# Recommendation scorer on one core: transposes of a pair of chunks in one PSUM tile of two banks, pooled sums copied by two pairs, one store at the end

## Chip, core and metric

The kernel runs on one core of one Trainium2 chip. The metric is device time in microseconds (us), the median of four executions. The engines are called as in the profile: PE is TensorE's matmuls and PEld its weight loads, DVE is VectorE, ACT is ScalarE, POOL is GpSimd, SP is SyncE. Beside the times there is one execution taken with the profiler, and every line of the trace is from that one.

## What is computed

A user has 69 item fields, a candidate item is the label, and both are rows of a table `emb` of 100001 x 96 floats. For every one of 16384 users:

```python
u = emb[batch_user]                       # 69 rows of 96
ql = emb[batch_label[:, 0]]               # 1 row
q = jnp.broadcast_to(ql[:, None, :], u.shape)
z = jnp.concatenate([q, u, q - u, q * u], axis=-1)
h = _dice(z @ W1 + b1, a1, EPS_DICE)      # 384 -> 64
h = h @ W2 + b2
att = h @ W3 + b3                         # one weight a field
eff = (batch_user < ITEM_NUM)[..., None]
pre = jnp.where(eff, u * att, 0.0)
pooled = jnp.einsum('gf,bfe->bge', window, pre).reshape(u.shape[0], G * E)   # 10 groups of fields
x = jnp.concatenate([pooled, ql], axis=-1)
h = _dice(_bn_eval(x @ Wf1 + bf1, EPS_BN), af1, EPS_DICE)                    # 1056 -> 200
h = _dice(_bn_eval(h @ Wf2 + bf2, EPS_BN), af2, EPS_DICE)                    # 200 -> 80
return h @ Wf3 + bf3
```

`_dice(x, a)` is `(a * (1 - p) + p) * x` with `p` the sigmoid of `x`.

## The kernel before

**Tiling.** The users are cut into 32 blocks of 512. Of the 69 fields, 64 are "main" and 5 are "tail". A chunk is 512 (user, field) places: a main chunk holds 8 users with all their 64 main fields, a tail chunk one tail field of all 512 users. A block has 64 main and 5 tail chunks. The loop runs over pairs of chunks, 69 x 32 / 2 = 1104 of them, and the order of all instructions is written by hand (`tc.manual_schedule()`); each engine runs its own instructions in that order and waits on semaphores for the others.

**A pair's way through the steps.** In step i:

- `seed(i-1)` (L278 to L295): a bf16 matmul of zeros opens a PSUM tile `ph`, and ACT copies into it the part of the hidden layer that depends on the label alone.
- `pool(i-8)` (L367 to L393): per chunk four matmuls with `u` as the stationary side and the attention weights `rw` as the moving one give the pooled sums `acc` in PSUM; DVE copies them into `pooled`. The `acc` tile exists once, so a pair's matmuls wait for the copy of the pair before.
- every fourth step `attend_rows` (L337, `prow`), and a step later `spread` (L353 `patt`, then DVE `w` at L356 and `rw` at L359) turn hidden values of four pairs into attention weights. Tail chunks go through `attend_tail` (L346, L347) instead.
- `hidden(i-2)` (L326 to L330): eight matmul records of `uT` and `quT` into `ph`, then sigmoid and an affine step on ACT and the product `y` on DVE.
- `fetch(i)` (L298 to L320): eight indirect DMAs by POOL (`gather`, L227) bring 128 rows each into `u`; PE transposes each (`ptr`, L308), four to a PSUM bank; per chunk DVE multiplies the bank by the label's row into `quT` (L311, for tail chunks L318) and ACT copies it into `uT` (L319).
- planned extra work: the loads of the next block's indices, its label's rows, and the dense tower of the block before in ten parts (`top1` L406 to L413 in eight, `top2` L420 to L424, `top3` L429 to L432, which also stores 512 results from SP's queue).

**Buffers.** `u` has 14 buffers (`upool`), `uT` and `quT` five each, `ps_tr` two banks, `ps_h` two, `ps_x` two, `ps_acc` one, `ps_m` one: eight PSUM banks in all. A gather needs its `u` buffer free, which is last read by `pool` eight steps after the fetch.

**Order in fetch.** A transpose is written straight after its gather, and each waits for that one gather:

```python
for t in range(4):
    gather(u[:, 4 * j + t, :], rows[n][:, 4 * k + t : 4 * k + t + 1])
    nc.tensor.transpose(ptr[:, t * P : (t + 1) * P], u[:, 4 * j + t, :], ident)
```

On POOL only gathers are queued, 8 for each pair and 4 more for each block's labels, 8960 in all.

Of the kernel before, what the change touches and what calls it, by code (L numbers as in the profile page):

```python
# [30 lines left out]
F32 = mybir.dt.float32  # L31
BF16 = mybir.dt.bfloat16
I32 = mybir.dt.int32
AF = mybir.ActivationFunctionType
ALU = mybir.AluOpType
PSUM = bass.MemoryType.PSUM

P = 128
B, F, E, G = 16384, 69, 96, 10
# [24 lines left out]
def rec_kernel(  # L64
# [23 lines left out]
    nc = tc.nc  # L88

    const = ctx.enter_context(tc.tile_pool(name="const", bufs=1))  # L90
# [7 lines left out]
    xpool = ctx.enter_context(tc.tile_pool(name="xpool", bufs=1))  # L98
# [31 lines left out]
    qTs = []  # L130
    for i in range(2):
        t = const.tile([E + 1, BLK + NS], F32, name=f"qT{i}")
# [47 lines left out]
    wf3 = const.tile([D2, 1], F32, name="wf3")  # L180
# [5 lines left out]
    bf3c = column(bf3, "bf3c", 1)  # L186
# [12 lines left out]

    with tc.tile_pool(name="prep_ps", bufs=1, space=PSUM) as pps:  # L200
        pv = pps.tile([P, E], F32, name="pv")
# [17 lines left out]
    def tail_weights(f):  # L219
        nc.vector.tensor_scalar_mul(V[:, f, :], wf1[:, 0, :], wr[:, f, 0:1])  # L220
        for g in range(1, G):
            nc.vector.scalar_tensor_tensor(
                V[:, f, :], wf1[:, g, :], wr[:, f, g : g + 1], V[:, f, :], ALU.mult, ALU.add
            )

    def gather(dst, index):
        nc.gpsimd.indirect_dma_start(  # L227
            out=dst,
            out_offset=None,
            in_=emb,  # L230
            in_offset=bass.IndirectOffsetOnAxis(ap=index, axis=0),
        )

    def chunk(c):

        return divmod(c, NCH)
# [33 lines left out]

    def by_field(ap):

        return ap.rearrange("e (s o) -> e s o", o=1).to_broadcast([ap.shape[0], NS, FM])

    def seed(i):

# [21 lines left out]
    def fetch(i):  # L298

        u = upool.tile([P, 8, E], F32, tag="u", name=f"u{i}")  # L300
        uT = tpool.tile([E, 2, 512], F32, tag="uT", name=f"uT{i}")
        quT = tpool.tile([E, 2, 512], F32, tag="quT", name=f"quT{i}")
        for j in range(2):
            n, k = chunk(2 * i + j)
            ptr = ps_tr.tile([E, 512], F32, tag="tr", name=f"ptr{i}_{j}")
            for t in range(4):
                gather(u[:, 4 * j + t, :], rows[n][:, 4 * k + t : 4 * k + t + 1])
                nc.tensor.transpose(ptr[:, t * P : (t + 1) * P], u[:, 4 * j + t, :], ident)  # L308
            q = qTs[n % 2][0:E]
            if k < NMAIN:  # L310
                nc.vector.tensor_tensor(  # L311
                    quT[:, j, :].rearrange("e (s f) -> e s f", f=FM),
                    ptr.rearrange("e (s f) -> e s f", f=FM),
                    by_field(q[:, k * NS : (k + 1) * NS]),
                    ALU.mult,
                )
            else:
                nc.vector.tensor_tensor(quT[:, j, :], ptr, q[:, 0:BLK], ALU.mult)  # L318
            nc.scalar.copy(uT[:, j, :], ptr)  # L319
        return u, uT, quT  # L320

    def hidden(i, ph, uT, quT):
# [19 lines left out]
    def attend_tail(i, j, y, uT):  # L342
# [3 lines left out]
        nc.tensor.matmul(pa, vrep[j * H1 : (j + 1) * H1, :], y[j * H1 : (j + 1) * H1, :], start=True, stop=True)  # L346
        nc.vector.scalar_tensor_tensor(pres[n][:, k - NMAIN, :], pa, bb[0:E], uT[:, j, :], ALU.add, ALU.mult)  # L347

    def spread(b, row):
# [14 lines left out]
        )  # L364
        return rw

    def pool(i, u, rw):  # L367

        todo = [(j, *chunk(2 * i + j)) for j in range(2)]
        todo = [(j, n, k) for j, n, k in todo if k < NMAIN]  # L370
        if not todo:
            return
        pa = ps_acc.tile([E, 2, NS, G], F32, tag="acc", name=f"acc{i}")
        for j, n, k in todo:
            for t in range(4):
                nc.tensor.matmul(  # L376
                    pa[:, j, 2 * t : 2 * t + 2, :].rearrange("e n g -> e (n g)"),
                    u[:, 4 * j + t, :],
                    rw[:, i % 4, j, t, :],
                    start=True,  # L380
                    stop=True,
                )
        if len(todo) == 2:
            _, n, k = todo[0]
            nc.vector.tensor_copy(  # L385
                pooled[n][:, :, k * NS : (k + 2) * NS].rearrange("e g s -> e s g"),
                pa.rearrange("e j s g -> e (j s) g"),
            )
        else:
            j, n, k = todo[0]  # L390
            nc.vector.tensor_copy(
                pooled[n][:, :, k * NS : (k + 1) * NS].rearrange("e g s -> e s g"), pa[:, j]
            )  # L393

    KTOP = G + 1 + NTAIL
# [29 lines left out]
        return x2  # L425

    def top3(n, x2):
        p3 = ps_m.tile([1, BLK], F32, tag="m", name=f"p3_{n}")
        nc.tensor.matmul(p3, wf3, x2, start=True, stop=True)  # L429
        res = xpool.tile([1, BLK], F32, tag="res", name=f"res{n}")  # L430
        nc.vector.tensor_scalar(res, p3, bf3c, None, ALU.add)
        nc.sync.dma_start(out=out_v[n : n + 1], in_=res)  # L432

    out_v = out.rearrange("(n b) o -> n (o b)", n=NBLK)

    cs, pooled, pres, x1s, x2s, qs, us, hs, phs, ys, bands, rws, p1s = ({} for _ in range(13))

# [32 lines left out]
    with tc.manual_schedule():  # L470
        qs[0] = head_gather(0)
        head_turn(0, qs.pop(0))
        cs[0] = head_row(0)
        for i in range(NPAIR + POOL_LAG + 16):
            if 0 <= i - 1 < NPAIR:
                phs[i - 1] = seed(i - 1)
            if 0 <= i - POOL_LAG < NPAIR:
                k = i - POOL_LAG
                pool(k, us.pop(k), rws[k // 4])
                if k % 4 == 3:  # L480
                    rws.pop(k // 4)
            if 0 <= i - 3 < NPAIR and (i - 3) % 4 == 3:
                b = (i - 3) // 4
                bands[b] = attend_rows(b, [ys[4 * b + k] for k in range(4)])
            if 0 <= i - 3 < NPAIR:
                k = i - 3
                uT = hs.pop(k)[0]
                for j in range(2):
                    if chunk(2 * k + j)[1] >= NMAIN:
                        attend_tail(k, j, ys[k], uT)  # L490
            if 0 <= i - 4 < NPAIR and (i - 4) % 4 == 3:
                b = (i - 4) // 4
                rws[b] = spread(b, bands.pop(b))
# [12 lines left out]
            for work in plan.pop(i, []):  # L506
                work()
    assert not plan


# [45 lines left out]
```

## Time and profile before

| what | us |
|---|---|
| median of four executions | 11338.62 |
| lowest, highest | 11337.48, 11348.81 |
| profiled execution, its own time | 11343.88 |
| its span, first to last instruction | 11342.1 |
| PE busy, idle waiting for gathered rows at L308 | 9833.1, 1292.8 |
| POOL busy | 8529.2 |
| DVE busy, ACT busy | 3191.8, 3761.1 |
| mean granted TensorE clock | 0.699 |

A line of costly groups reads: line, engine, operation, out<-in, shapes and count, then busy time and mean ns of one, then the idle time of the engine just before these instructions and what ended most of it. "Issue" is time in which an engine waited for nothing that the profile shows. A line of the timeline reads: start, duration, engine, line, operation, names, shapes, count, and in brackets the idle time before it with the one that ended it. A matmul of fp32 leaves two records, a transpose one.

Three groups that the change touches, from the costliest groups of the page:

```profile
L319 ACT COPY uT<-ptr 96x512 f32<-96x512 f32 x2208 | 1283.3, 581 | 2328.6 <-DVE quT L311 2151.6
...
L311 DVE TENSOR_TENSOR quT<-ptr,qT 96x512 f32<-96x512 f32 x2048 | 1352.6, 679 | 720.1 <-PE ptr L308 715.1
L385 DVE COPY pooled<-acc 96x160 f32<-96x160 f32 x1008 | 433.2, 430 | 2251.9 <-PE acc L376 2250.6
```

ACT spends 2151.6 us idle before the copies of `ptr`, until the DVE product of the same bank is done, since the two read one after the other.

### The profile page before, as it was taken

Reading aid. Unit: us, or ns where it says so; the run is one execution under the profiler, and the core shown is the slowest. Engines: PE = TensorE matmul, PEld = TensorE weight load, DVE = VectorE, ACT = ScalarE, POOL = GpSimd, SP = SyncE. Lnnn points to the kernel's source line nnn. Section 1 sums busy time; section 2 is a strip of 40 time slices with the busy share of each in tenths; the row PEclk is TensorE's granted clock in tenths of the full one; section 3 lists DMA queues with packets and bytes.
Section 4 is the critical chain, followed back from the end, with each engine's and each line's share of the span. In section 5 each row is a group of like instructions: output and inputs, shape, how many; then the busy total and the mean of one; then the engine's idle time right before and its main releaser. Section 6 shows DMA issues by size and latency. Waiting matters only on the chain.

```text
span 11342.1 us, 108113 instructions
## 1 busy us (share of the span) xinstructions
PE 9833.1 (87%) x41348; PEld 4777.8 (42%) x41348; DVE 3191.8 (28%) x5424; ACT 3761.1 (33%) x6086; POOL 8529.2 (75%) x8966
## 2 busy tenths in 40 slices
PE   7888888888888888888888888888888888888888
PEld 3444444444444444444444444444444444444444
DVE  3222222222222222222222222222222222222222
ACT  2333333333333333333333333333333333333332
POOL 7777777777777777777777777777777777777775
PEclk6766777667776677766767667777677766777767
DMA  1111111111111111111111111111111111111111
GB/s 44 40 41 40 40 40 40 40 40 40 40 40 40 40 40 40 40 40 40 40 40 40 40 40 40 40 40 40 40 40 40 40 40 40 40 40 40 40 40 29
DMA packets 295008, 453.59 MB, mean 40 GB/s; under 512 B 145952, under 2 KB 151104, under 8 KB 294496
## 3 DMA queue, kind: packets, MB, share of 16 engines
q0 software_dynamic: 286720, 440.98, 16.2%
q8 instruction: 331, 5.42, 0.2%
q1 hardware_dynamic: 6142, 4.77, 0.2%
q14 instruction: 181, 1.48, 0.0%
q10 hardware_dynamic: 1634, 0.94, 0.0%
HBM read 446.04 MB, written 0.07 MB: 39 GB/s over the span
## 4 chain that ended last, share of the span: by engine, by line
PE 33%; POOL 33%; DMA 18%; issue 12%; ACT 2%; DVE 1%; POOLq 0%; ACTq 0%
POOL u L227 32%; DMA u<-in_emb,rows 18%; PE ph L326 11%; PE acc L376 9%; PE p L406 4%; PE ptr L308 3%; PE prow L337 2%; PE ph L278 2%; POOL q L227 1%; ACT y L329 1%; PE pa L346 1%; PE patt L353 1%; DVE y L330 1%; ACT y L328 1%; PE pc L267 0%
## 5 line engine op out<-in xcount | busy, mean ns | idle before, releaser
L227 POOL DMA_INDIRECT u<-in_emb,rows x8832 | 8407.5, 952 | 2691.5 <-issue 2267.9
L308 PE MATMUL ptr<-ident,u 128*96 128x128 f32 x8832 | 2080.8, 358 | 1306.3 <-DMA u<-in_emb,rows 1292.8
L308 PEld LDWEIGHTS ptr<-ident,u 128*96 128x96 f32 x8832 | 1238.9, 157 | 3253.6 <-DMA u<-in_emb,rows 1679.5
L376 PEld LDWEIGHTS acc<-rw,u 128*96 128x96 f32 x16384 | 2073.9, 220 | 507.5 <-issue 506.9
L376 PE MATMUL acc<-rw,u 128*96 128x20 f32 x16384 | 2185.8, 284 | 1.8 <-DVE rw L359 1.3
L319 ACT COPY uT<-ptr 96x512 f32<-96x512 f32 x2208 | 1283.3, 581 | 2328.6 <-DVE quT L311 2151.6
L330 DVE TENSOR_TENSOR y<-ph,y 128x512 f32<-128x512 f32 x1104 | 763.7, 692 | 4443.3 <-ACT y L329 4341.6
L328 ACT ACTIVATE y<-ph 128x512 f32<-128x512 f32 x1104 | 659.2, 597 | 3855.9 <-PE ph L326 3855.6
L326 PE MATMUL ph<-uT,A 96*64 96x512 f32 x4416 | 1812.7, 913 | 0.0
L326 PE MATMUL ph<-quT,w 96*64 96x512 f32 x4416 | 1701.5, 861 | 0.0
L311 DVE TENSOR_TENSOR quT<-ptr,qT 96x512 f32<-96x512 f32 x2048 | 1352.6, 679 | 720.1 <-PE ptr L308 715.1
L385 DVE COPY pooled<-acc 96x160 f32<-96x160 f32 x1008 | 433.2, 430 | 2251.9 <-PE acc L376 2250.6
L329 ACT ACTIVATE y<-y,a1c,na1c 128x512 f32<-128x512 f32 x1104 | 897.4, 813 | 36.6
L326 PEld LDWEIGHTS ph<-quT,w 96*64 96x64 f32 x4416 | 448.1, 196 | 1088.5 <-issue 1088.5
L281 ACT COPY ph<-cT 128x512 f32<-128x512 f32 x1008 | 591.2, 586 | 449.0 <-PE ph L278 447.1
L278 PE MATMUL ph<-zrow 1*128 1x512 bf16 x1104 | 529.3, 479 | 163.4 <-DVE y L330 161.3
L406 PE MATMUL p<-pooled,wf 96*100 96x512 f32 x1280 | 665.3, 665 | 1.2 <-DVE x L410 0.8
L326 PEld LDWEIGHTS ph<-uT,A 96*64 96x64 f32 x4416 | 284.1, 178 | 540.8 <-issue 451.3
L337 PE MATMUL prow<-y,v 128*32 128x512 f32 x2208 | 443.9, 889 | 0.0
L339 ACT COPY row<-prow 128x512 f32<-128x512 f32 x276 | 161.5, 585 | 596.5 <-PE prow L337 595.2
L406 PEld LDWEIGHTS p<-pooled,wf 96*100 96x100 f32 x1280 | 233.9, 192 | 289.1 <-issue 286.9
L278 PEld LDWEIGHTS <-zrow 1*128 1x128 bf16 x1104 | 104.1, 94 | 477.1 <-issue 453.0
(71 smaller groups left out, 2651.0 us busy)
## 6 DMA issues: line engine op xcount, KB each, us to landing
u<-in_emb,rows POOLq DMA_INDIRECT x8832, 2.4
ids<-in_idx SPq DMA_DIRECT2D x32, 140.0 KB
q<-in_emb,ids POOLq DMA_INDIRECT x128, 2.4
wf<-in_Wf ACTq DMA_DIRECT2D x1, 825.0 KB
out<-res SPq DMA_DIRECT2D x32, 2.0 KB
w<-in_W SPq DMA_DIRECT2D x1, 96.0 KB
wf<-in_Wf ACTq DMA_DIRECT2D x1, 62.5 KB
a1c<-in_a SPq DMA_DIRECT2D x2, 0.2 KB
```

The source lines that it names most:

```text
L227: nc.gpsimd.indirect_dma_start(out=dst, out_offset=None, in_=emb, in_offset=bass.IndirectOffsetOnAxis(ap=index, axis=0),)
L278: nc.tensor.matmul(ph, zrow[:, 0:P], zrow, start=True, stop=False)
L308: nc.tensor.transpose(ptr[:, t * P : (t + 1) * P], u[:, 4 * j + t, :], ident)
L311: nc.vector.tensor_tensor(quT[:, j, :].rearrange("e (s f) -> e s f", f=FM), ptr.rearrange("e (s f) -> e s f", f=FM), by_field(q[:, k * NS ...
L319: nc.scalar.copy(uT[:, j, :], ptr)
L326: nc.tensor.matmul(ph[j * H1 : (j + 1) * H1, :], w, x[:, j, :], start=False, stop=last)
L328: nc.scalar.activation(y, ph, AF.Sigmoid, scale=S_DICE)
L329: nc.scalar.activation(y, y, AF.Identity, bias=a1c, scale=na1c)
L330: nc.vector.tensor_mul(y, ph, y)
L337: nc.tensor.matmul(pr[32 * k : 32 * (k + 1), :], v2, y, start=True, stop=True)
L376: nc.tensor.matmul(pa[:, j, 2 * t : 2 * t + 2, :].rearrange("e n g -> e (n g)"), u[:, 4 * j + t, :], rw[:, i % 4, j, t, :], start=True, st ...
L406: nc.tensor.matmul(p1, w[:, h * DH : (h + 1) * DH], x, start=(k == 0), stop=(k == KTOP - 1))
```

## The change

All eight gathers of a pair are written first, then the eight transposes into one PSUM tile `ptr` of two banks, of which there is now one (`ps_tr` has one buffer of two banks instead of two of one). The first transpose waits for all eight gathers through dependencies added by hand; the others have no wait. One DVE product and one ACT copy read both banks; only where a pair lies in two blocks or has a main and a tail chunk are there two DVE products.

`pool` opens an `acc` tile at even pairs, writes the next pair's sums beside it, and copies both at the odd pair, as one DVE copy for each block they belong to.

`top3` makes its 512 results with `x2` as the stationary side, four matmuls of one column each, into 4 columns of a tile `res` of 128 x 128 in SBUF that holds all results. `store()` at the end transposes `res`, copies it and stores all 16384 results in one DMA. The bias `bf3` is loaded broadcast to 128 partitions.

```diff
+    bf3c = const.tile([P, 1], F32, name="bf3c")
+    nc.sync.dma_start(out=bf3c, in_=bf3.rearrange("(o n) -> o n", o=1).to_broadcast([P, 1]))
+    res = const.tile([P, NBLK * NQ], F32, name="res")
...
-    ps_tr = ctx.enter_context(tc.tile_pool(name="ps_tr", bufs=2, space=PSUM))
+    ps_tr = ctx.enter_context(tc.tile_pool(name="ps_tr", bufs=1, space=PSUM))
...
+        sources = []
         for j in range(2):
             n, k = chunk(2 * i + j)
-            ptr = ps_tr.tile([E, 512], F32, tag="tr", name=f"ptr{i}_{j}")
             for t in range(4):
-                gather(u[:, 4 * j + t, :], rows[n][:, 4 * k + t : 4 * k + t + 1])
-                nc.tensor.transpose(ptr[:, t * P : (t + 1) * P], u[:, 4 * j + t, :], ident)
...
+                sources.append(gather(u[:, 4 * j + t, :], rows[n][:, 4 * k + t : 4 * k + t + 1]))
+        ptr = ps_tr.tile([E, 2, 512], F32, tag="tr", name=f"ptr{i}")
+        for t in range(8):
+            turn = nc.tensor.transpose(
+                ptr.rearrange("e j x -> e (j x)")[:, t * P : (t + 1) * P], u[:, t, :], ident
+            )
+            if t == 0:
+
+                for source in sources[1:]:
+                    tc.add_manual_dep(turn.ins, source.ins.name, SYNC)
+        (n0, k0), (n1, k1) = chunk(2 * i), chunk(2 * i + 1)
+        q = qTs[n0 % 2][0:E]
+        if n0 == n1 and k1 < NMAIN:
+            nc.vector.tensor_tensor(
+                quT.rearrange("e j (s f) -> e (j s) f", f=FM),
+                ptr.rearrange("e j (s f) -> e (j s) f", f=FM),
+                by_field(q[:, k0 * NS : (k0 + 2) * NS]),
+                ALU.mult,
+            )
...
+        nc.scalar.copy(uT, ptr)
         return u, uT, quT
...
+        if i % 2 == 0:
+            accs[0] = ps_acc.tile([E, 4, NS, G], F32, tag="acc", name=f"acc{i}")
+        pa = accs[0]
+        for j in range(2):
+            if chunk(2 * i + j)[1] < NMAIN:
+                for t in range(4):
+                    nc.tensor.matmul(
+                        pa[:, 2 * (i % 2) + j, 2 * t : 2 * t + 2, :].rearrange("e n g -> e (n g)"),
...
+        if i % 2 == 0:
             return
...
+        for block in sorted({n for n, k in places if k < NMAIN}):
+            m = [m for m, (n, k) in enumerate(places) if n == block and k < NMAIN]
+            k = places[m[0]][1]
             nc.vector.tensor_copy(
+                pooled[block][:, :, k * NS : (k + len(m)) * NS].rearrange("e g s -> e s g"),
+                pa[:, m[0] : m[-1] + 1].rearrange("e m s g -> e (m s) g"),
             )
...
     def top3(n, x2):
-        p3 = ps_m.tile([1, BLK], F32, tag="m", name=f"p3_{n}")
-        nc.tensor.matmul(p3, wf3, x2, start=True, stop=True)
-        res = xpool.tile([1, BLK], F32, tag="res", name=f"res{n}")
-        nc.vector.tensor_scalar(res, p3, bf3c, None, ALU.add)
-        nc.sync.dma_start(out=out_v[n : n + 1], in_=res)
...
+        p3 = ps_m.tile([P, NQ], F32, tag="m", name=f"p3_{n}")
+        for k in range(NQ):
+            nc.tensor.matmul(p3[:, k : k + 1], x2[:, k * P : (k + 1) * P], wf3, start=True, stop=True)
+        nc.vector.tensor_scalar(res[:, n * NQ : (n + 1) * NQ], p3, bf3c, None, ALU.add)
+
+    def store():
+        p4 = ps_m.tile([NBLK * NQ, P], F32, tag="m", name="p4")
+        nc.tensor.transpose(p4, res, ident)
+        r = xpool.tile([NBLK * NQ, P], F32, tag="g1", name="r")
+        nc.vector.tensor_copy(r, p4)
+        nc.sync.dma_start(out=out.rearrange("(m p) o -> m (p o)", p=P), in_=r)
```

More of the change, by code (lines that the diff above doesn't have):

```diff
@@ L35 @@
 ALU = mybir.AluOpType
+SYNC = mybir.DependencyInfo(mybir.DependencyClass.Sync, mybir.DependencyReason.DATA)
 PSUM = bass.MemoryType.PSUM
@@ L185, in rec_kernel @@
     af2c = column(af2, "af2c", D2)
-    bf3c = column(bf3, "bf3c", 1)
+    bf3c = const.tile([P, 1], F32, name="bf3c")
+    nc.sync.dma_start(out=bf3c, in_=bf3.rearrange("(o n) -> o n", o=1).to_broadcast([P, 1]))
+    res = const.tile([P, NBLK * NQ], F32, name="res")
     naf1c = [one_minus(t, f"naf1c{i}") for i, t in enumerate(af1c)]
@@ L226, in gather @@
     def gather(dst, index):
-        nc.gpsimd.indirect_dma_start(
+        return nc.gpsimd.indirect_dma_start(
             out=dst,
@@ L271, in by_field @@
     def by_field(ap):
-        return ap.rearrange("e (s o) -> e s o", o=1).to_broadcast([ap.shape[0], NS, FM])
+        return ap.rearrange("e (s o) -> e s o", o=1).to_broadcast([ap.shape[0], ap.shape[1], FM])
     def seed(i):
@@ L302, in fetch @@
         quT = tpool.tile([E, 2, 512], F32, tag="quT", name=f"quT{i}")
+        sources = []
         for j in range(2):
             n, k = chunk(2 * i + j)
-            ptr = ps_tr.tile([E, 512], F32, tag="tr", name=f"ptr{i}_{j}")
             for t in range(4):
-                gather(u[:, 4 * j + t, :], rows[n][:, 4 * k + t : 4 * k + t + 1])
[L308 to L318, printed above, removed]
@@ L319, in fetch @@
-            nc.scalar.copy(uT[:, j, :], ptr)
+                sources.append(gather(u[:, 4 * j + t, :], rows[n][:, 4 * k + t : 4 * k + t + 1]))
[7 more added lines that the diff above has]
+                    tc.add_manual_dep(turn.ins, source.ins.name, SYNC)
@@ new lines, in fetch @@
+        (n0, k0), (n1, k1) = chunk(2 * i), chunk(2 * i + 1)
[7 more added lines that the diff above has]
+            )
+        elif n0 == n1 and k0 >= NMAIN:
+            nc.vector.tensor_tensor(
+                quT, ptr, q[:, 0:BLK].rearrange("e (o x) -> e o x", o=1).to_broadcast([E, 2, BLK]), ALU.mult
+            )
+        else:
+            for j, (n, k) in enumerate([(n0, k0), (n1, k1)]):
+                q = qTs[n % 2][0:E]
+                if k < NMAIN:
+                    nc.vector.tensor_tensor(
+                        quT[:, j, :].rearrange("e (s f) -> e s f", f=FM),
+                        ptr[:, j, :].rearrange("e (s f) -> e s f", f=FM),
+                        by_field(q[:, k * NS : (k + 1) * NS]),
+                        ALU.mult,
+                    )
+                else:
+                    nc.vector.tensor_tensor(quT[:, j, :], ptr[:, j, :], q[:, 0:BLK], ALU.mult)
@@ L365, in spread @@
         return rw
+    accs = {}
     def pool(i, u, rw):
-        todo = [(j, *chunk(2 * i + j)) for j in range(2)]
-        todo = [(j, n, k) for j, n, k in todo if k < NMAIN]
-        if not todo:
-            return
[L373 to L384, printed above, removed]
-            nc.vector.tensor_copy(
[L386 to L392, printed above, removed]
+        if i % 2 == 0:
[6 more added lines that the diff above has]
+                        pa[:, 2 * (i % 2) + j, 2 * t : 2 * t + 2, :].rearrange("e n g -> e (n g)"),
+                        u[:, 4 * j + t, :],
+                        rw[:, i % 4, j, t, :],
+                        start=True,
+                        stop=True,
+                    )
+        if i % 2 == 0:
+            return
+        places = [chunk(2 * i - 2 + m) for m in range(4)]
+        for block in sorted({n for n, k in places if k < NMAIN}):
+            m = [m for m, (n, k) in enumerate(places) if n == block and k < NMAIN]
+            k = places[m[0]][1]
+            nc.vector.tensor_copy(
+                pooled[block][:, :, k * NS : (k + len(m)) * NS].rearrange("e g s -> e s g"),
+                pa[:, m[0] : m[-1] + 1].rearrange("e m s g -> e (m s) g"),
             )
@@ L427, in top3 @@
     def top3(n, x2):
-        p3 = ps_m.tile([1, BLK], F32, tag="m", name=f"p3_{n}")
-        nc.tensor.matmul(p3, wf3, x2, start=True, stop=True)
-        res = xpool.tile([1, BLK], F32, tag="res", name=f"res{n}")
-        nc.vector.tensor_scalar(res, p3, bf3c, None, ALU.add)
-        nc.sync.dma_start(out=out_v[n : n + 1], in_=res)
-    out_v = out.rearrange("(n b) o -> n (o b)", n=NBLK)
+        p3 = ps_m.tile([P, NQ], F32, tag="m", name=f"p3_{n}")
[8 more added lines that the diff above has]
+        nc.sync.dma_start(out=out.rearrange("(m p) o -> m (p o)", p=P), in_=r)
     cs, pooled, pres, x1s, x2s, qs, us, hs, phs, ys, bands, rws, p1s = ({} for _ in range(13))
@@ L507, in rec_kernel @@
                 work()
+        store()
     assert not plan
```

## The prediction

> **What bounds the kernel now.** I read the page first: its busy table, its chain and the costliest groups. Then I read what GpSimd (POOL) waits for, all accesses to the gathered tile u, the timeline of two stretches, and last the end of the kernel.
>
> ```profile
> span 11342.1 us, 108113 instructions
> ...
> PE 9833.1 (87%) x41348; PEld 4777.8 (42%) x41348; DVE 3191.8 (28%) x5424; ACT 3761.1 (33%) x6086; POOL 8529.2 (75%) x8966
> ...
> PE 33%; POOL 33%; DMA 18%; issue 12%; ACT 2%; DVE 1%; POOLq 0%; ACTq 0%
> ...
> L227 POOL DMA_INDIRECT u<-in_emb,rows x8832 | 8407.5, 952 | 2691.5 <-issue 2267.9
> L308 PE MATMUL ptr<-ident,u 128*96 128x128 f32 x8832 | 2080.8, 358 | 1306.3 <-DMA u<-in_emb,rows 1292.8
> ```
>
> What GpSimd waits for (total us, times, longest us):
>
> ```profile
> POOL u L227 <- issue: 2267.9, 7442, 0.3
> POOL u L227 <- DMA u<-in_emb,rows: 294.4, 966, 0.3
> ```
>
> TensorE at 87% looks like the bound, but it sat idle 1293 us waiting for gathered rows. GpSimd looks 75% busy. Yet no pause before a gather is longer than 0.3 us, whatever is named as its releaser: that pause is the price of issuing the next one. Read from the trace gather by gather: 8960 gathers (8832 of u, 128 of q), the first starting at 3.19 us, the last ending at 11261.90; pauses of 0.303 to 0.313 us, sum 8959 x 0.3047 = 2730.2; durations 8528.5 us. Both together are 11258.7, exactly that stretch. So GpSimd never waits for another engine, and the chain's steps through TensorE are guesses of its releaser rule. The kernel is 3.2 us of start, 11258.7 us of gathers, 80.2 us of end.
>
> The durations hold one thing that other engines touch. All but 210 gathers take 0.94 us; those 210 take up to 1.596 and are 73.7 us too long in sum. Two places show why:
>
> ```profile
> 5020.91 0.82 DVE L359 TENSOR_TENSOR rw<-R,w 128x640 f32<-128x640 f32 x1
> 5021.05 1.50 POOL L227 DMA_INDIRECT u<-in_emb,rows  x1 [0.30 <-issue]
> ...
> 5087.73 1.27 DVE L311 TENSOR_TENSOR quT<-ptr,qT 96x512 f32<-96x512 f32 x2
> 5087.77 0.94 POOL L227 DMA_INDIRECT u<-in_emb,rows  x1 [0.30 <-DMA u<-in_emb,rows]
> ...
> 5092.61 0.69 DVE L413 TENSOR_TENSOR x<-x,g 100x512 f32<-100x512 f32 x1 [1.54 <-ACT g L412]
> 5092.76 1.36 POOL L227 DMA_INDIRECT u<-in_emb,rows  x1 [0.30 <-issue]
> ```
>
> A gather that starts while a VectorE operation with both inputs in SBUF runs (rw, x) ends 0.94 us after about 0.1 us before that operation's end. A VectorE operation that reads PSUM (quT) costs it nothing. An SBUF operation that starts after the gather has begun costs nothing either. By operation, the 73.7 us are: rw (L359, 276 of them) 48, x (L413, 64) 21, the rest (L424, L222, L108) under 5.
>
> [...] here the ScalarE copy of ptr waits for the VectorE product (uT starts 0.03 us after quT ends).[...] the trace shows a mean of 0.699, 0.99 in the dense 5080 to 5096 us and 0.50 in the end up to 11299.
>
> **The change, part by part.**
>
> *Gathers.* The order of instructions shows the same 8960 on GpSimd, in the same order with the same kinds of waits. 8960 x 0.9436 + 2730.2 = 11185 us stay; no edit shortens them.
>
> *One read of a pair.* 2208 ScalarE copies of 0.581 become 1104;[...] The pooled copy of two pairs (L385 took 0.430 for 160 elements, L391 0.293 for 80, so 1.7 ns each) comes to 0.70 against 2 x 0.43. [...] worth 0, as GpSimd waits for neither. All of these read PSUM, so none stalls a gather.
>
> *The wait for eight landings.* Today seven transposes slip in between landings and only the eighth comes after the last one (in 5085.53 to 5086.54 seven are done early). Now all eight follow it. Behind the first on TensorE stand the other seven, the dense tower's part of that step, the seed, the pooling and the hidden matmuls; VectorE and ScalarE wait for the results. So all of that moves later by seven transposes: 7 x 0.214 = 1.5 us at the half clock (x4 in 1.09), 0.107 each or 0.75 us at full. One ptr tile instead of two costs nothing: its two readers are done some 2.4 us after the last transpose, and the next pair's first comes some 7 us later. GpSimd is far away: u has 14 buffers and is last read by the pooling 8 steps on, leaving 5 steps x 10.2 us = 51 us before a late TensorE stops a gather. Cost 0; if the cover fails, rival D.
>
> *Which VectorE operations now meet a gather.* This is where the time can move. For L413 the lock is tight: in 57 of 64 cases it starts 6.08 us after the step's last transpose, which starts as its gather lands (2.43 us after its issue). 6.08 + 2.43 + 0.04 = 8.55 us, less 6 gather periods of 1.249, puts it 1.06 us into a period, just before the next gather: 0.36 us lost each time. Adding 0.75 gives 1.81 - 1.25 = 0.56: it ends 0.0 us past the next start, before the 0.1 us at which a gather is hurt. Eight waits in a row on TensorE are not in the trace; at 0 to 0.3 us they move it to 0.86 at most, 0.2 us of loss. So 21 us become 0 to 13; I take 4, minus 17. For rw (L359) the distance from the last transpose to its start spreads from 2.9 to 8.1 us (5th to 95th percentile), over four periods, because the clock differs from step to step. It is hurtful to start between 0.55 and 1.2 us into a period, with a loss from 0 to 0.65 us; evenly spread, that is 0.65 x 0.65 / (2 x 1.249) = 0.17 us each, 276 x 0.17 = 47, as today. Shifting each of the 276 by its own seven transposes at its own clock gives 0.85 of today's loss, 41. I take 44 between the two: minus 4. L424 and the rest: minus 1. Sum minus 22. Bounds: rw all clear, minus 48; rw all at the bad place, 276 x 0.45 = 124, plus 76.
>
> *Blocks and stores.* 31 stores leave SP's queue, which otherwise only loads ids some 20 steps ahead: 0. The broadcast load of bf3c stands ahead of the second ids load, not needed for 20 steps: 0.
>
> *The end.*
>
> ```profile
> 11262.23 1.94 PE L308 MATMUL ptr<-ident,u 128*96 128x128 f32 x8
> ...
> 11264.56 0.58 PE L278 MATMUL ph<-zrow 1*128 1x512 bf16 x1 [0.39 <-DVE y L330]
> ...
> 11337.18 1.88 PE p L429 x2
> 11339.08 0.74 DVE res L431
> ```
>
> The last gather, issued at 11260.96, lands at 11263.4; eight transposes now begin there and end at 11265.3, so the seed starts 0.8 later. Two copies between the last pooling matmuls become one: minus 0.3. The last layer and store take 1.88 + 0.74 + 2.3 to the end = 4.9. After: eight short loads and matmuls at 0.17 (16 of acc take 2.68) 1.3, res 0.2, transpose 0.5, copy of 128x128 0.3 (vrep took 0.26), semaphores 0.2, and 64 KB stored in 2.3 to 3.0 (a gather of 48 KB lands in 2.4), 2.5: 5.0. Sum plus 0.6, I take plus 1. The clock there may differ: 36 us at half could be 18 shorter.
>
> Sum: minus 22 plus 1 = minus 21 on the span of 11342.1, 11321. The profiled execution took 11343.88, 1.8 more than its span and 5.3 over the median 11338.62 of the four; the same minus 21 off the median gives **11317 us**. A measurement here tells 0.2% (22.7 us) from no change: the forecast lies close to that line.
>
> **Rivals.**
> A, the forecast: rw stays scattered. 11317, own range 11290 to 11340, chance 0.62.
> B, rw falls between the gathers. For it: at a steady half clock the sum of rows (2.43 + transposes 1.9 + seed 0.5 + acc 2.6 + patt 1.1 + w 0.3 = 8.8, less 7 periods) is 0.1 into a gather, harmless. Against: the spread of four periods. rw costs 10 instead of 44: 11283. Chance 0.15.
> C, slower: the opposite lock. TensorE now waits once a step and starts anew from the same landing; at full clock the sum (2.43 + 0.95 + 0.3 + 1.5 + 0.65 + 0.3 = 6.1, less 4 periods) is 1.1 into a period, the worst place. rw at 0.45 each: 11338.6 - 18 + 1 + 76 = 11398. It passes the old time once rw averages (48 + 17) / 276 = 0.24 us, and is measurably slower from 0.32. Chance 0.13.
> D, TensorE becomes the bound. At the half clock a step takes 8.7 (transposes, seed, acc, ph) + 0.7 (prow, patt) + 2.1 (tower, head, tail fields) = 11.5 us against 10.2. Always: 1104 x 1.3, 12770 us; a quarter of the time, 11700. Against: [...]a step then fits: 9.3 us with a part of the tower and prow in it (first transpose at 5085.53 to the next step's at 5094.86), some 5 without. Chance 0.06.
> E, nothing visible: the instructions merge as the diff says, but the collisions stay as they are: 11339. Chance 0.04.
>
> **Numbers.** Faster: nearly half of A (0.30) and B, 0.45. Same: 0.31 of A and E, 0.35. Slower: C, D and 0.01 of A, 0.20. The range 11280 to 11370 holds A, most of B and the near end of C; D, the rest of C and B's far end, 0.20, lie outside.
>
> **What would show it.** Still 8960 gathers with pauses of 0.30 us and a median of 0.944; if any pause exceeds 0.35 us, D. No gather over 1.05 us beside x<-x,g, or that step is wrong. The sum of long gathers near 50 us; 12 is B, 120 is C. An end of 81 us from the last gather.[...]

## The result: 14 us faster, 0.12%

The changed kernel took 11329.43 us (median of 40 runs, 11322.35 to 11339.43). The kernel before took 11343.08 on the same chip (60 runs, 11335.1 to 11352.61). The ratio is 0.9988 [0.9983, 0.9992], minus 13.65 us. The interval leaves out 1, so the gain is real, but it is smaller than the 0.2% that the prediction took for the least that can be told from no change. It lies inside the range given, 11280 to 11370. The profiled execution took 11331.77 us, its span is 11329.9, 12.2 less than the span before.

The page of the changed kernel, its totals, its chain and its costliest groups:

```profile
span 11329.9 us, 107996 instructions
...
PE 9548.3 (84%) x41541; PEld 4980.8 (44%) x41541; DVE 3013.2 (27%) x3849; ACT 3581.2 (32%) x4982; POOL 8515.8 (75%) x8966
...
POOL 39%; PE 26%; DMA 16%; issue 15%; ACT 2%; DVE 1%; POOLq 0%; ACTq 0%
...
L230 POOL DMA_INDIRECT u<-in_emb,rows x8832 | 8393.4, 950 | 2691.5 <-issue 2364.8
L313 PE MATMUL ptr<-ident,u 128*96 128x128 f32 x8832 | 1730.0, 362 | 1519.9 <-DMA u<-in_emb,rows 728.1
...
L345 ACT COPY uT<-ptr 96x1024 f32<-96x1024 f32 x1104 | 1112.0, 1007 | 3279.9 <-DVE quT L323 2973.6
...
L323 DVE TENSOR_TENSOR quT<-ptr,qT 96x1024 f32<-96x1024 f32 x1008 | 1225.5, 1216 | 1027.4 <-PE ptr L313 1024.5
```

The counts follow the diff. VectorE issues 3849 instructions instead of 5424, ScalarE 4982 instead of 6086, and TensorE is busy 285 us less. None of it shows in the time. What the span follows is the first two figures of the L230 row, 8393.4 busy and 2691.5 idle before it, and of these only the busy time moved. What GpSimd waits for (total us, times, longest us):

```profile
POOL u L230 <- issue: 2364.8, 7760, 0.3
POOL u L230 <- DMA u<-in_emb,rows: 291.3, 956, 0.3
```

The longest pause is still 0.3 us, so GpSimd still waits for nobody. Gather by gather (a long gather is one over the usual length, its excess what it takes beyond that; a hit is a gather made long by the operation named):

| part of the span, us | before | after |
|---|---|---|
| before the first gather | 3.2 | 3.3 |
| 8960 gathers at the usual length | 0.94358 each | 0.94354 each |
| pauses, mean | 0.30474 | 0.30475 |
| long gathers, excess in sum | 74.0 | 60.8 |
| of it beside rw | 48.1 | 47.5 |
| of it beside the first x<-x,g | 21.2 (58 hits) | 7.8 (28 hits) |
| of it beside the second x<-x,g | 1.4 | 2.9 |
| first gather's start to last one's end | 11258.7 | 11245.3 |
| after the last gather | 80.2 | 81.3 |

Between the two profiled executions there are thus minus 13.4 us in the gathers and plus 1.2 at both ends. Nearly all of the minus 13.4 is the excess of long gathers (minus 13.2), and that comes from one VectorE operation, x<-x,g of the first hidden layer, which now starts at another place between two gathers. This is an account of two traces: no run undid the shift of x alone in an undisturbed execution (see the last experiment). Two stretches of the changed kernel's timeline (start us, us, engine and operation, in brackets the idle time before it):

```profile
525.17 0.69 DVE L440 TENSOR_TENSOR x<-x,g 100x512 f32<-100x512 f32 x1 [1.54 <-ACT g L439]
525.38 1.30 POOL L230 DMA_INDIRECT u<-in_emb,rows  x1 [0.30 <-issue]
...
4737.64 0.94 POOL L230 DMA_INDIRECT u<-in_emb,rows  x1 [0.30 <-issue]
...
4738.20 0.69 DVE L440 TENSOR_TENSOR x<-x,g 100x512 f32<-100x512 f32 x1 [1.54 <-ACT g L439]
...
4738.89 0.94 POOL L230 DMA_INDIRECT u<-in_emb,rows  x1 [0.30 <-issue]
```

At 4738.20 x starts 0.56 us into a period and ends just as the next gather starts: nothing is lost. At 525.17 it starts 0.21 us ahead of the next gather, which takes 1.30 instead of 0.94. The two steps differ in how long the dense tower's products ahead of x took on TensorE; the first line is of the step of 525.17, the second of that of 4738.20:

```profile
517.73 5.11 PE L433 MATMUL p<-pre,V 96*100 96x512 f32 x8
...
4732.27 3.60 PE L433 MATMUL p<-pre,V 96*100 96x512 f32 x8
```

The section on the prediction comes back to this. The chain that ended last, over the last 80 us (start us, us, step):

```profile
11247.65 2.47 DMA u<-in_emb,rows
11250.12 0.14 issue
11250.25 1.92 PE ptr L313 x8
...
11285.42 0.57 DVE pooled L417
...
11324.29 1.88 PE p L457 x8
...
11326.19 0.23 DVE res L458
...
11326.47 0.49 PE p L462
...
11326.98 0.29 DVE r L464
```

The eight transposes stand after the last landing as one block of 1.92 us. The last layer and the single store, from 11324.29 to the end at 11329.9, take 5.6 us.

### The profile page after: what moved, and what is told of

It reads as the page before. It is cut to its first block, busy times and chain, and to the rows that moved or that the text cites. A ratio compares the mean times of both kernels' runs of the same rounds, so it can differ in the third digit from the quotient of the medians.

```text
span 11329.9 us, 107996 instructions
## 1 busy us (share of the span) xinstructions
PE 9548.3 (84%) x41541; PEld 4980.8 (44%) x41541; DVE 3013.2 (27%) x3849; ACT 3581.2 (32%) x4982; POOL 8515.8 (75%) x8966
## 4 chain that ended last, share of the span: by engine, by line
POOL 39%; PE 26%; DMA 16%; issue 15%; ACT 2%; DVE 1%; POOLq 0%; ACTq 0%
POOL u L230 39%; DMA u<-in_emb,rows 16%; PE ph L352 8%; PE acc L403 6%; PE p L433 4%; PE ptr L313 4%; PE ph L281 1%; ACT y L354 1%; PE prow L363 1%; ACT y L355 1%; PE pa L372 1%; DVE y L356 1%; POOL q L230 1%; PE patt L379 1%; PE p L457 0%
## 5 line engine op out<-in xcount | busy, mean ns | idle before, releaser
L230 POOL DMA_INDIRECT u<-in_emb,rows x8832 | 8393.4, 950 | 2691.5 <-issue 2364.8
L313 PE MATMUL ptr<-ident,u 128*96 128x128 f32 x8832 | 1730.0, 362 | 1519.9 <-DMA u<-in_emb,rows 728.1
L313 PEld LDWEIGHTS ptr<-ident,u 128*96 128x96 f32 x8832 | 1324.5, 168 | 2959.3 <-issue 1697.8
L403 PEld LDWEIGHTS acc<-rw,u 128*96 128x96 f32 x16384 | 2125.7, 225 | 574.9 <-issue 574.9
L403 PE MATMUL acc<-rw,u 128*96 128x20 f32 x16384 | 2237.8, 288 | 1.3 <-DVE rw L385 1.3
L345 ACT COPY uT<-ptr 96x1024 f32<-96x1024 f32 x1104 | 1112.0, 1007 | 3279.9 <-DVE quT L323 2973.6
L352 PE MATMUL ph<-uT,A 96*64 96x512 f32 x4416 | 1788.9, 902 | 0.0
L352 PE MATMUL ph<-quT,w 96*64 96x512 f32 x4416 | 1668.1, 846 | 0.0
L323 DVE TENSOR_TENSOR quT<-ptr,qT 96x1024 f32<-96x1024 f32 x1008 | 1225.5, 1216 | 1027.4 <-PE ptr L313 1024.5
L417 DVE COPY pooled<-acc 96x320 f32<-96x320 f32 (+3 forms) x536 | 363.5, 678 | 1003.0 <-PE acc L403 1002.6
```

Of the source, the lines that this page charges most:

```text
L230: return nc.gpsimd.indirect_dma_start(out=dst, out_offset=None, in_=emb, in_offset=bass.IndirectOffsetOnAxis(ap=index, axis=0),)
L313: turn = nc.tensor.transpose(ptr.rearrange("e j x -> e (j x)")[:, t * P : (t + 1) * P], u[:, t, :], ident)
L323: nc.vector.tensor_tensor(quT.rearrange("e j (s f) -> e (j s) f", f=FM), ptr.rearrange("e j (s f) -> e (j s) f", f=FM), by_field(q[:, k0 * ...
L345: nc.scalar.copy(uT, ptr)
L352: nc.tensor.matmul(ph[j * H1 : (j + 1) * H1, :], w, x[:, j, :], start=False, stop=last)
L403: nc.tensor.matmul(pa[:, 2 * (i % 2) + j, 2 * t : 2 * t + 2, :].rearrange("e n g -> e (n g)"), u[:, 4 * j + t, :], rw[:, i % 4, j, t, :], ...
```

## The experiments

The theory: GpSimd's gathers are the span, and the only thing that other engines can do to them is to run a VectorE operation with both inputs in SBUF at a gather's start. Rival 1: the long gathers have some other cause (any busy VectorE, a DMA in the way), and taking those operations off SBUF changes nothing. Rival 2: fetch and pooling matter by themselves, because TensorE or the cover of the u buffers is near its limit.

The runs came from three chips. On the first, the kernel before took 11362.93 us (19 runs), and each ratio below is to that. The changed kernel itself did not run there, so a comparison with it is one of two ratios, and a difference of two ratios is known to within 0.0010 to 0.0014, 11 to 16 us. On the other two chips the kernel before took 13428.8 and 13596.59: TensorE, VectorE and ScalarE stood still together there now and then with nothing recorded to wait for (up to 29.4 us before a weight load of acc in the trace shown below). What those runs can tell is said with them.

### The stall: one operand from PSUM

In the changed kernel w is written back into the PSUM bank of patt, so that rw reads one input from PSUM. The values are the same.

```diff
-        w = rpool.tile([P, 4, 2, 4], F32, tag="w", name=f"w{b}")
+        w = pt.rearrange("p t k j -> p (t k j)").rearrange("p (m o) -> p m o", o=16)[:, :, 4:5]
...
+            w.to_broadcast([P, 32, 2 * G]),
             R.rearrange("p (k g) -> p k g", k=1).to_broadcast([P, 32, 2 * G]),
-            w.rearrange("p k j (t o) -> p (k j t) o", o=1).to_broadcast([P, 32, 2 * G]),
```

> The changed kernel with w written back into PSUM (beside patt), so that rw<-w,R reads one input from PSUM, as quT does; same results, same count of operations. Theory (a gather is stalled by a VectorE operation with both inputs in SBUF): no gather beside rw is long any more, minus 47 us, about 11282. Rival (any VectorE operation as long as this one stalls a gather, or its length does): no gain, 11329[...].

Measured: 11299.95 us (5 runs), ratio 0.9944 [0.993, 0.9957]. Against the changed kernel (0.9988) that is 0.0044 less, some 50 us (34 to 66 by the intervals), where 47.5 stood beside rw. All accesses to rw in this kernel (ns min/median/max, first and last start, form):

```profile
L389 DVE TENSOR_TENSOR rw<-patt,R x276: 824/825/826, 87.5 to 11247.8; 128x640 f32<-128x640 f32 x138
```

The operation is as long as before (its median was 826 ns). How gathers meet it, in the changed kernel:

```profile
1142.85 0.82 DVE L385 TENSOR_TENSOR rw<-R,w 128x640 f32<-128x640 f32 x1
1142.94 1.56 POOL L230 DMA_INDIRECT u<-in_emb,rows  x1 [0.30 <-issue]
```

and in the experiment:

```profile
251.14 0.82 DVE L389 TENSOR_TENSOR rw<-patt,R 128x640 f32<-128x640 f32 x1
251.22 0.95 POOL L230 DMA_INDIRECT u<-in_emb,rows  x1 [0.30 <-issue]
```

In both the gather starts 0.08 to 0.09 us after rw. With both inputs in SBUF it loses 0.62 us, with one in PSUM nothing. The sum of long gathers falls from 60.8 to 11.0, with 0 beside rw and 8.1 beside x. Rival 1 is out for rw: it isn't VectorE's being busy, nor the operation's length, but where its second input lies. The absolute time is above the expected 11282 because the usual gather took 945.8 ns in the profiled execution instead of 943.5 (last section).

### The same for the tower's products

In addition the sigmoid and the product of the two hidden layers read the layer's sums straight from PSUM, with the constants scaled once at the start.

```diff
-        nc.vector.tensor_scalar(x1, p1, S_BN, sbf1[h], ALU.mult, ALU.add)
-        nc.scalar.activation(g1, x1, AF.Sigmoid, scale=S_DICE)
-        nc.scalar.activation(g1, g1, AF.Identity, bias=af1c[h], scale=naf1c[h])
-        nc.vector.tensor_mul(x1, x1, g1)
+        sb, sa, sn = tower[h]
+        nc.scalar.activation(g1, p1, AF.Sigmoid, bias=sb, scale=S_BN * S_DICE)
+        nc.scalar.activation(g1, g1, AF.Identity, bias=sa, scale=sn)
+        nc.vector.scalar_tensor_tensor(x1, p1, bf1c[h], g1, ALU.add, ALU.mult)
```

> As the run before, and in the tower ScalarE's sigmoid and VectorE's product read the matmul's sums from PSUM (scale and bias of the normalisation go into ScalarE's constants and the product's added bias), so x<-x,g and its like no longer have two SBUF inputs. Theory: about 10 us more go, 11272; the long gathers that stay are those of the 45 V operations and 32 rows operations, 3 us in sum; the end within 2 us of 81. Rival: as the run before, 11282, if x<-x,g was not to blame.

Measured: 11301.57 us (5 runs, 11278.7 to 11301.87), ratio 0.9945 [0.9932, 0.9959], the same as the run above. In the profiled executions the excess did fall, from 11.0 to 2.8. But the end from the last gather grew from 75.9 to 86.7 us, so the 8 us were lost where no gather runs (the expectation was an end within 2 us of 81). In that end the granted clock was lower than in the run above (0.51, 0.74 and 0.74 in its three equal stretches, where the run above has 0.61, 0.86 and 0.90), and TensorE is busy in 72.5 of the end's 87 us. Why the clock was lower there stays open. The costliest group of the two experiments, first rw alone:

```profile
L230 POOL DMA_INDIRECT u<-in_emb,rows x8832 | 8364.1, 947 | 2692.9 <-issue 2342.6
```

then with the tower's products as well:

```profile
L240 POOL DMA_INDIRECT u<-in_emb,rows x8832 | 8335.8, 944 | 2691.5 <-issue 2352.0
```

The 28 us between them are 8 of excess and some 20 of the usual length, 945.8 against 943.5 ns in these two executions: a row of the costliest groups can differ for a reason that isn't in the kernel.

### The suspected cost doubled

In the changed kernel rw is written twice, by the same instruction.

> The changed kernel with the operation rw done twice in a row, 276 more VectorE operations of 0.83 us. Theory: [...]rw's 47 us of stalls double, 11377; if it doesn't, each pair acts as one operation of 1.65 us, which always lies over a gather's start, 0.95 us lost on average, 11545. Rival (VectorE's time is hidden, stalls come from elsewhere): 11329.

Measured: 11397.58 us (6 runs), ratio 1.0032 [1.002, 1.0044], 0.0044 (some 50 us) above the changed kernel, the mirror image of the PSUM run. Excess 103.9: the first rw 46.1, the second 44.3, x 10.3. VectorE is busy 29% of the time and no pause of GpSimd is over 0.35 us; within the 15 us to which the comparison is known, the 276 added operations (0.82 us each, 228 us of work) cost what the gathers lose beside them and no more. No gather takes over 1.6 us, so a waiting gather gets in between the two. A price of 0.16 to 0.17 us for each such operation at an arbitrary moment held for both.

### The cover: nine u buffers

```diff
-    upool = ctx.enter_context(tc.tile_pool(name="upool", bufs=14))
+    upool = ctx.enter_context(tc.tile_pool(name="upool", bufs=9))
```

> The changed kernel with 9 instead of 14 buffers of u. A gather then needs the pooling of the step just before, which is done some 2.4 us ahead of it when TensorE is on time. Theory (with 14 buffers TensorE's lateness is covered by 5 steps): now it shows, some 5 to 10% of pairs make GpSimd pause by 1 to 5 us before their first gather, 50 to 200 us more, 11380 to 11530. Rival (TensorE's lateness never matters): no pause over 0.35 us, 11329.

Measured: 11375.34 us (12 runs), ratio 1.001 [1.0002, 1.0019]. Against the changed kernel's 0.9988 that is 0.0022, 25 us. GpSimd's waits:

```profile
POOL u L230 <- issue: 2350.2, 7708, 0.3
POOL u L230 <- DMA u<-in_emb,rows: 291.2, 955, 0.3
...
POOL u L230 <- PE acc L403: 35.6, 40, 1.4
```

and one of them on the timeline:

```profile
3665.28 0.95 POOL L230 DMA_INDIRECT u<-in_emb,rows  x1 [0.30 <-issue]
3667.63 0.95 POOL L230 DMA_INDIRECT u<-in_emb,rows  x1 [1.40 <-PE acc L403]
```

Now a pause ends with the pooling matmuls. 35 pauses are longer than 0.35 us and cost 23.3 us, nearly all of the 25. With 14 buffers there is none, so there the work moved later on TensorE is hidden, as forecast; even with no step of cover left only 3% of the 1104 pairs come too late, by 0.67 us each. The expectation was two to eight times that.

### The parts by themselves

Six kernels separate the parts of the change. In the first the gathers and transposes of a pair alternate again, without the wait for eight, into the pair's one tile:

```diff
-                sources.append(gather(u[:, 4 * j + t, :], rows[n][:, 4 * k + t : 4 * k + t + 1]))
...
+                gather(u[:, 4 * j + t, :], rows[n][:, 4 * k + t : 4 * k + t + 1])
+                nc.tensor.transpose(ptr[:, j, t * P : (t + 1) * P], u[:, 4 * j + t, :], ident)
```

> The changed kernel, but each transpose again waits for its own gather alone; the pair's tile, its single reads, the pooled copies and the one store stay. Theory (only VectorE's SBUF operations that lie on the start of a gather matter, and the wait for eight landings moved x<-x,g off it): the last transpose starts at the landing again, x<-x,g is again 1.06 us into a gather period, its loss is about 20 us instead of 7.8, rw stays near 48, so the time goes back to about 11343 us, 13 above the changed kernel. Rival (reading a pair at once saves time): it stays at 11329. Rival (one store and pair copies): it stays at 11329.

In the second the wait stays and each bank is read by operations of its own:

```diff
-        nc.scalar.copy(uT, ptr)
...
+            nc.scalar.copy(uT[:, j, :], ptr[:, j, :])
```

> The changed kernel with the wait for eight landings, but two VectorE products and two ScalarE copies a pair again, some 0.3 us more work a pair on two engines. Theory: GpSimd waits for neither, 11329 us (within 8), gathers unchanged, x<-x,g loses 5 to 10. Rival (the single reads save the time): back to about 11343.

The third is the kernel before with the one store at the end alone (its `top3` and `store` are those of the diff above):

> The kernel before with the new last layer and the single store alone. Theory: nothing on GpSimd moves; x<-x,g still loses about 21 us, the sum of long gathers stays at 70 to 76, the end 80 us: 11343 us. Rival (31 stores fewer help): some 10 us faster.

The fourth is the kernel before with the pooled sums copied by two pairs alone (its `pool` is that of the diff above):

> The kernel before with the pooled sums copied by two pairs alone. Theory: the copies read PSUM and stall no gather; 11343 us, the end 0.3 us shorter, x<-x,g still at about 21 us. Rival (fewer VectorE operations free time): some 10 us faster.

| kernel | time us | ratio | excess beside rw, first + second x |
|---|---|---|---|
| alternating waits | 13448.15 | 1.0009 [0.9996, 1.0022] | 57.1, 3.9 + 3.0 |
| two reads a pair | 13442.91 | 1.0006 [0.9994, 1.0018] | 43.5, 6.2 + 4.7 |
| store alone | 13440.88 | 1.0009 [0.9996, 1.0021] | 49.6, 7.6 + 3.3 |
| pooled copies alone | 13435.76 | 1.0005 [0.9986, 1.0024] | 59.5, 5.5 + 3.8 |

The kernel before took 13428.8 us on this chip. None of the four can be told from it, but the intervals are as wide as the 0.12% in question. The first two ran again on the third chip, with two others beside them.

> The changed kernel, but each transpose waits for its own gather alone again; the pair's tile, its single reads, the pooled copies and the one store stay. Theory (the wait for eight landings moved x<-x,g off the start of a gather): the step's last transpose starts at the landing again, x<-x,g (64 of them) loses about 20 us instead of 7.8, rw near 48 (35 to 60, its places are scattered), ratio to the kernel before 0.999 to 1.001. Rival (reading a pair at once, or the other parts, save the time): x<-x,g below 10 us and ratio 0.9988.

> The changed kernel with the wait for eight landings, but two VectorE products and two ScalarE copies a pair again. Theory: GpSimd waits for neither engine; no pause over 0.35 us, x<-x,g loses 5 to 10 us, ratio to the kernel before 0.998 to 0.9995. Rival (the single reads save the time): x<-x,g may stay low but the ratio is 1.000.

Both edits on the kernel before together, store and pooled copies, with the fetch as it was:

> The kernel before with the new last layer and single store and the pooled sums copied by two pairs; the fetch is the old one. Theory: none of it stalls or frees a gather; x<-x,g loses about 21 us, rw 35 to 60, the end 80 us, ratio to the kernel before 0.9995 to 1.0005. Rival (these parts bring the gain): ratio 0.9988.

The kernel before with rw and the tower's products reading PSUM as in the two experiments above (the recorded text calls that no-lock):

> The kernel before, with rw and the tower's products reading PSUM as in the no-lock kernel, and none of the change under study. Theory (the change acts only through such stalls): the sum of long gathers falls to about 3 us, the gathers' stretch to 11188 us within 2, the same as of the changed kernel without the lock (11190.3 at its last gather's end); ratio to the kernel before about 0.9938, the end's clock apart. Rival (the change also saves something that does not come from such stalls): the last gather ends over 5 us later than there.

| kernel | time us | ratio | excess beside rw, first + second x |
|---|---|---|---|
| alternating waits | 13558.44 | 0.9966 [0.995, 0.9982] | 35.1, 4.9 + 2.2 |
| two reads a pair | 13624.55 | 1.0027 [1.0013, 1.0041] | 55.1, 8.1 + 4.7 |
| store and pooled copies | 13573.38 | 0.9975 [0.9962, 0.9988] | 55.2, 8.1 + 1.8 |
| before, rw and x from PSUM | 13666.91 | 1.0047 [1.0033, 1.006] | 0, 0 |

These ratios settle nothing: the same kernel with alternating waits is at 1.0009 on the second chip and at 0.9966 on the third, that with two reads a pair at 1.0006 and 1.0027. The waits in the trace of the alternating one on the third chip (total us, times, longest us) show why:

```profile
PEld acc L395 <- issue: 2693.1, 1039, 29.4
POOL u L230 <- issue: 2378.3, 7792, 0.6
...
ACT y L346 <- remote: 1706.0, 205, 24.1
...
POOL u L230 <- PE acc L395: 995.9, 196, 42.8
...
POOL u L230 <- remote: 670.9, 201, 6.1
```

The second line is the usual price of issuing. The others aren't there in the result's kernel: weight loads of acc stood 575 us for "issue" there and stand 2693 here, and pauses that end with acc or "remote" (a releaser outside the program) come to 1667 us. TensorE runs 60 us and more behind the landings in nine steps of ten, more than the u buffers cover, and then GpSimd waits for it: 656 pauses, 2191 us. This is rival D's regime. The kernel before is in it as well, by its times on these chips and by the trace of its variant with rw and x reading PSUM, so the change didn't bring it. What makes the engines stand still stays open.

Two things can still be read there. The stalls vanish in the old fetch too: with rw and x reading PSUM the kernel before has an excess of 2.2 us in sum. And x has no fixed place any more while TensorE is too late to wait for landings: old and new forms of fetch all show 3.9 to 8.1 us, where some 20 were expected of the old ones. The time of each part in an undisturbed execution was thus not measured. That the reads, pooled copies and store gave nothing rests on the trace alone: they end in no wait of GpSimd, whose pauses are unchanged.

## Why the prediction came out as it did

**The bound.** Right, and shown: removing 47.5 us of stalls on GpSimd took some 50 us off the time and doubling them added as much. 1575 fewer VectorE and 1104 fewer ScalarE instructions took off no more than the 13 us by which the long gathers became shorter.

**One read of a pair, at 0.** Right by the trace, not measured alone. quT takes 1.216 us where two took 2 x 0.679, uT 1.007 where two took 2 x 0.581. pooled takes 0.70 for two pairs (forecast 0.70). All three read PSUM, and so does y: of the 1540 gathers of the changed kernel that start beside quT, pooled or y, 1538 take at most 0.96 us (in the other two, of 1.04 and 1.07, the operation rows starts at 0.91 and 0.94 us).

**The wait for eight landings, at 0 on the path.** Right: no pause over 0.308 us. Two transposes that follow one another are 0.213 us apart where the granted clock is 0.50 and 0.109 where it is 1.00 (medians, changed kernel; forecast 0.214 and 0.107). The run with nine buffers shows what the cover is worth.

**The shift of x.** Right in kind, mis-sized by 4 us: hits fell from 58 to 28 of 64, but 7.8 us stayed where 4 were forecast. "No gather over 1.05 us beside x" did not come true. Two terms were off.

The first is the wait of the first transpose, which I let range from 0 to 0.3 us and put near its low end. In the trace it has two values. Where the last gather of the pair signals on one DMA semaphore, the first transpose starts a median 0.14 us after the landing (573 pairs); where it signals on another, 0.41 us (531 pairs). In the first case x mostly starts 0.55 to 0.70 us into a period and costs nothing, in the second mostly 0.85 to 1.0, and costs 0.17 to 0.31; the 21 hits of this kind make 5.1 us.

The second is a term that the prediction put at nothing: it kept the distance from the last transpose to x at its old value. It is 6.04 us (6.08 before) in 48 of the 64 cases only, against 58 before. In 14 cases, against 4 before, it is 7.0 to 7.8, because the tower's products ran slower: their eight records took 4.4 to 5.3 us at a granted clock of 0.68 to 0.81, instead of 3.60 at 1.00. The two lines shown with the result are of 0.70 and 1.00. Seven of these x then start at 1.0 to 1.1 us into a period, like those of the kernel before, and cost 2.6 us; the other seven pass beyond the start of the gather and cost nothing. The three other runs with the wait for eight on the undisturbed chip whose x still reads SBUF have 7 to 15 such cases. Why the clock falls more often there no run shows.

The likely cause of the two values of the wait stands in the order of instructions: the eight waits are spread over four wait instructions of 51 ns with two each and the transpose itself, and which comes where is fixed, while the four gathers of a block's labels move the pairs on by four semaphores from one block to the next. In every other block the last landing is thus waited for early in the row, and the rest of the row follows after it. The trace has it so: in nearly all pairs one wait instruction comes after the last landing in the first kind and three, 0.106 us apart, in the second; two of these distances are 0.21 of the 0.27 us between the kinds. Runs with the wait for eight on the undisturbed chip show the same remainder (7.4 and 7.8 with rw read from PSUM and written twice; 5.3 with nine buffers). No run changed the order of the waits, so it stays the likely cause.

**rw, minus 4.** Too hopeful by 3.5 us: 47.5 stayed of 48.1. In the changed kernel it starts from 2.9 to 7.5 us after the last transpose (5th to 95th percentile), still over almost four periods; an even spread (47 by the prediction's own formula) was the better guess than shifting each start by seven transposes. The second x lost 1.5 us more instead of 1 less.

**The end, plus 1.** 81.3 against 80.2, right in sum. The last layer and store took 5.6 instead of 5.0: the eight loads and matmuls are 1.88 us, as long as the two before, not 1.3. It was made up elsewhere in the end.

**The sum.** Forecast minus 21 on the span, measured minus 12.2 on it and minus 13.65 in the medians. The difference on the span is 4 us of x, 3.5 of rw and 2.5 of the second x, less about 1 beside smaller operations. Of the rivals, B and C (rw clear of the gathers, or locked to their starts) fell with rw at 47.5, D with the pauses (longest 0.308 us), E with x at 7.8. How the granted clock follows the load of TensorE, on which D depends, no trace shows: in the kernel before it was 0.99 from 5080 to 5096 us, with TensorE busy in 15.9 of 16 us, and 0.50 from 11265 to 11299, with 31.8 of 34. Forecast A came true at its weaker end, and a gain over 0.2%, which I held likelier than none, didn't come. The range given also held no gain at all (11339), so the number alone says little for the prediction; what speaks for it is that the gain came where it was looked for, in the hits of x.

**A faster version.** rw from PSUM in the changed kernel: ratio 0.9944 [0.993, 0.9957]. Against the changed kernel this small edit brings nearly four times what the whole change brought.

## What to carry over

Where gathers on GpSimd are back to back and never wait, merging reads, copies and stores on the other engines saved nothing here that the trace shows, however many instructions went; look at which gathers are longer than the rest and what runs at their start. A VectorE operation with two SBUF inputs, rw, at a random moment cost 0.17 us of GpSimd here, and giving it one input from PSUM removed that at no cost in its own length (0.825 us against 0.826; x, as another instruction, went from 0.69 to 0.75). A change that only shifts such an operation can win or lose its stall by a tenth of a microsecond, so forecast it as a spread, not as a place.

## What was not expected of the hardware

**Who delays whom.** The two delay each other unequally. In 170 hits of the changed kernel, of rw and x, the gather is late by the time from its start to the operation's end, less 0.13 us. A gather that has started first doesn't delay rw in this way; in the changed kernel:

```profile
254.07 0.89 DVE L385 TENSOR_TENSOR rw<-R,w 128x640 f32<-128x640 f32 x1
254.10 0.94 POOL L230 DMA_INDIRECT u<-in_emb,rows  x1 [0.30 <-issue]
```

With rw only 0.03 us ahead the gather is not hurt, and rw takes 0.89 instead of 0.83. The edge is sharp. An rw that starts 0.044 us ahead of a gather makes it take 1.598; one that starts 0.042 ahead leaves it at 0.940 and takes 0.899 itself, the longest in the kernel. From there the delay of rw shrinks to nothing at 0.03 us after the gather's start, and an rw that starts later in the gather's 0.94 us loses nothing (0.824 to 0.827 us in all 194 such cases). So a gather delays rw only in some 0.07 us close to its start, from 0.042 ahead of it to 0.03 after. Why, and why two SBUF inputs make a gather late, no run shows.

**Two lengths of a gather.** The usual gather takes 943.5 ns in some profiled executions and 945.8 in others, constant throughout one (three executions on the third chip show 944.0). Times of one kernel fall into two groups that fit this, 11278.7 and 11301.2 to 11301.9 for the kernel with rw and the tower's products reading PSUM: 2.3 ns and 0.15 ns of pause, times 8960, make 22 us, more than the change itself. Of these only the one of 11278.7 has a trace, with 943.5; that the others have 945.8 is inferred from the 22 us. The two profiled executions of the result both have 943.5, so their difference is free of this.
